# Graph network, layer 2: maximum in place, four-node pieces, longer gaps, and three engines in written order

## The chip, the cores and the metric

The kernel runs on one core of one Trainium2 chip. The metric is the device time of one execution in microseconds (us); the figure for a kernel is the median of its runs. The core has five engines, each with an instruction queue of its own: TensorE (PE in the profile, with its weight loads as PEld), VectorE (DVE), ScalarE (ACT), GpSimd (POOL) and SyncE (SP). DMAs are issued by SP, ACT and POOL.

## The reference, cut to what matters

Four graph layers run on N = 6250 nodes (49 tiles of 128) with E = 100000 edges (782 groups of 128), sorted by destination. The input is normalised, and the result is added to it at the end.

```python
h = jnp.maximum(_layernorm(x), 0.0)
msum = segment_sum(h[src], dst)                                        # layer 1: mean
h = h @ W1_self + (msum / clip(deg, 1)) @ W1_neigh + b1
hp = relu(h @ W2_pool + b2_pool)                                       # layer 2: maximum
hmax = where(deg > 0, segment_max(hp[src], dst), 0.0)
h = h @ W2_self + hmax @ W2_neigh + b2
h = ((segment_sum(h[src], dst) + h) / (deg + 1)) @ W3_neigh + b3       # layer 3: gcn
h = h @ W4_self + (segment_sum(h[src], dst) / clip(deg, 1)) @ W4_neigh + b4
out = x + h @ W_fc + b_fc
```

The destinations are skewed: low node numbers have far more edges than high ones.

## The kernel before

The kernel has a fast path, timed here, and a general path that runs only when a flag says that the graph doesn't fit the fast one. Because the layers after the maximum are linear, the fast path folds the weights of layers 2 to 4 together; `W3_neigh`, `W4_*` and `W_fc` are multiplied into products of 256 or 512 columns, and layers 3 and 4 only add up rows.

Neighbour sums of layers 1, 3 and 4 are done in two ways. For the tiles of nodes with many edges (hub tiles, numbers 0 to `HUB`: 8, 16 or 18 by layer) the adjacency is a dense table `A` of small counts, multiplied by the rows on TensorE (`dense`, L489). For the others the edges are gathered 128 at a time and added up by one-hot products (`sums`). `build` makes the dense tables: nodes are taken in windows of `WIN = 8`; each group of up to 128 edges of a window becomes two one-hot matrices, `hs` (source within its tile; two ScalarE operations, L319 and L321) and `hm` (source tile and node of the window; VectorE, L323), whose product (L329) counts the edges. Windows of tiles 0 to 7 are built during layer 1, those of tiles 8 to 17 during layer 2, with two groups of edges each. After a layer-2 window's last product ScalarE runs over it twice: `many` (L337) looks whether a count exceeds 15 and L339 copies it into `A` as fp8. `Hub` holds such a list of work, makes the one-hots `LOOK = 4` ahead, and is moved on by `advance`.

Layer 2 is one long loop over the 782 groups of edges, in six blocks (`BLOCKS`), the last block first. In each step POOL gathers 128 rows of 512 floats by source (L1240) into half of a buffer `X` (six buffers of two halves), and VectorE keeps a running maximum along the edges of each lane (L1247), into two PSUM tiles `run0` and `run1` in turn. Of each pair one row is kept: a third VectorE operation makes it (L1283), and it is stored to DRAM (L1288). After a block `carry` joins the runs that cross from one lane to the next.

Beside this, in every step, the loop moves on several things, all in Python generators whose `yield` gives the turn back until the next step:

- `products2`, the weight folding: 28 pieces, from step 9 one per step. A piece of `product` loads 128 rows of weights (`wl`, issued by ScalarE), transposes them on TensorE (L259), copies them (L260), multiplies (L263) and copies the result (L265).
- `chains` and `node_rows`: keys for `carry` and, per block, the rows at which each node's maximum will lie.
- `hub.advance`: the windows of tiles 8 to 15 until step 250, of 16 and 17 after.
- `done2`, one per tile of nodes whose blocks are complete: gathers the maxima (`totals`, L1149), transposes, multiplies by the folded weights (L1173, L1176, L1179), adds the bias row `prow` (L1183) and writes the row in three bf16 parts (`parts`) to `tab_r`.
- `early`: the products of layer 3 with tiles 6 to 37 of `tab_r`, in batches of four tiles, that can be made already here; their sums go to `acc3` (`add3`, L1040).

The order in which an engine issues its instructions is chosen by a scheduler when the kernel is built: it works from the dependencies and its own estimate of durations, and may move instructions past one another. Once built, each engine's queue is fixed.

Of the kernel before, what the change touches and what calls it, by code (L numbers as in the profile page):

```python
# [20 lines left out]
P = 128  # L21
# [8 lines left out]
WIN = 8  # L30
# [48 lines left out]
def fast_path(  # L79
# [59 lines left out]
    WT = P // WIN  # L139
    NW = WT * H4  # L140
    assert H1 <= H3 <= H4 and NW + 1 <= 3 * P
    k_of = [math.ceil(_edges_between(w * WIN, (w + 1) * WIN, E, N) / P) for w in range(NW)]
    assert all(p >= q for p, q in zip(k_of, k_of[1:]))
    row_of, spans = {}, []
    nrow = 0
    for w0, w1_ in ((0, WT * H1), (WT * H1, NW)):
# [72 lines left out]
    most = const.tile([P, NW], F32, name="most")  # L219
# [86 lines left out]

    def build(d, A, keys, pool, psb, plain=True):

        sk, mk, r0 = keys
        work = []  # L310
        for w in range(d * WT, (d + 1) * WT):
            hold = {}
            for k in range(k_of[w]):
# [12 lines left out]
                def run(k=k, w=w, hots=hots, hold=hold):  # L326
# [4 lines left out]
                    if k == k_of[w] - 1:  # L331
                        c = (w % WT) * WIN
                        if plain:
                            nc.vector.tensor_reduce(most[:, w : w + 1], hold[0], AX.X, ALU.max)
                        else:
                            many = pool.tile([P, NT * WIN], BF16, name="many", bufs=1)
                            nc.scalar.activation(many, hold[0], AF.Relu, bias=less,  # L337
                                                 accum_out=most[:, w : w + 1])
# [8 lines left out]

    LOOK = 4

    class Hub:  # L350


        def __init__(self, work=()):
# [23 lines left out]
        def advance(self, to):  # L377
            while self.done < min(to, len(self.work)):
                if self.work[self.done][0]:
                    self.passed += 1  # L380
                while self.hot < min(self.passed + LOOK, len(self.hot_at)):
                    self.work[self.hot_at[self.hot]][0]()
                    self.hot += 1
# [194 lines left out]
    with ExitStack() as pro:  # L578
# [67 lines left out]
        for r, w0, n, k in spans:  # L646
# [6 lines left out]
        sel_at = (0, RB1, RB1)  # L653
        sel = [ep.tile([P, n], F32, name=f"sel{c}")
               for c, n in enumerate((RB1, RB * P - RB1, RB * P - RB1))]

        def select(c):
# [8 lines left out]
        iota_n = ep.tile([P, 3 * P], F16, name="iota_n")  # L666
        nc.gpsimd.iota(iota_n, pattern=[[WIN, 3 * P]], base=0, channel_multiplier=0,
                       allow_small_or_imprecise_dtypes=True)
        SN = ep.tile([P, 3, 2], F32, name="SN")
        nc.gpsimd.iota(SN[:, :, 1], pattern=[[WIN * P, 3]], base=0, channel_multiplier=WIN,  # L670
                       allow_small_or_imprecise_dtypes=True)
        dlast = ep.tile([P, 1], F32, name="dlastf")
        nc.vector.tensor_copy(dlast, dstI[:, T - 1 : T])
        under = ep.tile([P, 3 * P], BF16, name="under")
        nc.vector.tensor_scalar(under, iota_n, dlast, None, op0=ALU.is_gt)
        pc = bank(psm, "pm", "pc_c", (3,))
        for c in range(3):
            nc.tensor.matmul(pc[:, c : c + 1], under[:, c * P : (c + 1) * P], ones_b,
                             start=True, stop=True)
        cF = ep.tile([P, 3], F32, name="cF")  # L680
        nc.vector.tensor_scalar(cF, pc, float(P - 1), None, op0=ALU.min)
        cI = ep.tile([P, 3], I32, name="cI")
        nc.vector.tensor_copy(cI, cF)
        within = ep.tile([P, 3], F32, name="within")
# [28 lines left out]
        def check_room():  # L713

            pr_ = bank(psm, "pm", "pr_s", (3 * P,))
            for c in range(3):
                nc.tensor.matmul(pr_[:1, c * P : (c + 1) * P], SN[:, c, 0:1], ident,
                                 start=True, stop=True)
            starts = ep.tile([1, 3 * P], F32, name="starts")
# [40 lines left out]
        def window_keys(sk, mk):  # L760
# [5 lines left out]
            nc.vector.scalar_tensor_tensor(mk[:, c], mk[:, c], float(WIN) / P, dw[:, c],  # L766
                                           op0=ALU.mult, op1=ALU.add)
            nc.vector.tensor_scalar(dw[:, c], dw[:, c], float(WIN), 1024.0, op0=ALU.is_ge,
# [88 lines left out]
        window_keys(sk1, mk1)  # L857
        select(1)
        select(2)
        begins(1)  # L860
        begins(2)
        row_begins(RB1 // P, RB, (1, 2))
# [20 lines left out]
        window_keys(skR, mkR)  # L883
# [69 lines left out]
    def node_rows(pool, psm):  # L953
# [28 lines left out]
        for b, tb in enumerate(BLOCKS):  # L982
# [6 lines left out]
            nc.vector.tensor_mul(q, q, ok)  # L989
            nc.vector.tensor_scalar(pI, q, 1.0 / tb, None, op0=ALU.mult)  # L990
# [17 lines left out]
            nc.vector.tensor_add(t_, t_, pF)  # L1008
            nc.vector.tensor_scalar(t_, t_, float(run_at[b]), None, op0=ALU.add)
# [35 lines left out]
    with tc.tile_pool(name="fl2c", bufs=1) as ck, ExitStack() as late:  # L1045
# [3 lines left out]
        psb = late.enter_context(tc.tile_pool(name="psb2", bufs=1, space=PSUM))  # L1049
# [4 lines left out]
        prow = ck.tile([P, FH], F32, name="prowf")  # L1054
# [26 lines left out]
        def products2(wp):  # L1081
# [7 lines left out]
            b4r = wp.tile([P, FO], F32, name="b4rf")  # L1089
            b2r = wp.tile([P, FH], F32, name="b2rf")  # L1090
# [22 lines left out]
        def carry(b, last):  # L1113
# [3 lines left out]
            yield  # L1117
            cT = wk.tile([P, KH, P], F32, name="cTf", bufs=1)
# [8 lines left out]
            yield  # L1127
            pc = bank(psm, "pm", "pcf")
            for k in range(KH):
                nc.tensor.transpose(pc[:, k * P : (k + 1) * P], cT[:, k, :], ident)  # L1130
            for _ in range(4):
                yield
# [5 lines left out]
            for _ in range(4):  # L1138
                yield
# [18 lines left out]
        def done2(d):  # L1158
            tots, th = totals(d)
            for _ in range(4):  # L1160
                yield
# [5 lines left out]
            for j in range(KH):  # L1167
                nc.tensor.transpose(pt[:, j, :], hm[:, j * P : (j + 1) * P], ident)
            hT = wk.tile([P, KH, P], F32, name="hTf")
            nc.scalar.copy(hT, pt)  # L1170
            pm = bank(psm, "pm", "pm_prf")
# [10 lines left out]
            pr = wk.tile([P, FH], F32, name="prf")  # L1182
# [17 lines left out]
        early_pool = []  # L1200

        def early_products():
# [3 lines left out]
            for d in range(H3):  # L1206
                got = {}

                def load(d=d, got=got):
# [5 lines left out]
                             lambda s: batch[s], FH, psd, lambda v, d=d: add3(d, v))  # L1215
                early.add([(load, work[0])] + work[1:])
# [4 lines left out]
        A = wk.tile([P, NT, P], F8, name="A", bufs=1)  # L1221
        first, rest = (
            [w for d in ds for w in build(d, A, (skR, mkR, RB1), wk, psb, False)]
            for ds in (range(H1, H3), range(H3, H4))
        )
        hub = Hub(first + rest)
        tiles, begun2 = [], 0
# [3 lines left out]
        for b in reversed(range(NB)):  # L1231
            tb = BLOCKS[b]
            t0 = offs[b] // P
            prev = None
            for s0 in range(0, tb, G2):
                n = min(G2, tb - s0)
                X = (xmore if at // G2 % 2 else xpool).tile([P, G2, FH], F32, name="X2")
                for k in range(n):
# [5 lines left out]
                    if s0 + k:  # L1244
                        run = (X[:, k, :] if s0 + G2 >= tb
                               else psr.tile([P, FH], F32, name=f"run{k}"))
                        nc.vector.scalar_tensor_tensor(  # L1247
                            run, prev, same[:, t : t + 1], X[:, k, :],
                            op0=ALU.mult, op1=ALU.max,
# [828 lines left out]
```

## Time and profile before

| | |
|---|---|
| median of 3 runs | 3320.49 us (3316.07 to 3323.73) |
| the profiled execution | 3354.4 us |
| its span in the profile | 3352.6 us |
| mean granted TensorE clock | 0.885 |
| busy: PE, DVE, ACT, POOL | 2515.0, 2178.8, 993.2, 1948.2 us |
| HBM traffic | 806 MB, mean 240 GB/s |
| layer 1 (with the start), layer 2, layers 3 and 4 | about 0 to 910, 910 to 2335, 2335 to 3352 us |

The profile is of one execution. "Busy" is the time in which an engine executed instructions other than register, branch, semaphore and DMA-issuing ones. A line of a group gives: source line, engine, operation, output and inputs, shape, count, busy us, mean ns of one, and then the idle time of the engine just before them with what ended most of it. "issue" means that the engine waited for nothing that the profile shows. In the tables of windows each engine's busy time is followed by its number of instructions, and the last three columns are the granted TensorE clock as a share of full speed, the mean busy share of the 16 DMA engines, and GB/s.

### The profile page before, as it was taken

The page shows a single profiled execution, that of the slowest core. Times are in us where ns is not written, and L with a number is a line of the kernel's source. Part 1 is how long each engine was busy: PE and PEld are TensorE (multiplying, and loading weights), DVE is VectorE, ACT ScalarE, POOL GpSimd, SP SyncE. Part 2 cuts the span into 40 slices and gives each one's busy share as a digit, 9 for nine tenths or more (in the row PEclk, how much of TensorE's full clock was granted, in tenths as well). Part 3 has the DMA queues.
Part 4 walks back from the last instruction along what each step waited for, and adds up shares of the span by engine and source line. Part 5 has one row for each costly group of instructions (what it writes and reads, how often), then busy time and mean ns, then how long its engine had stood idle before and what let it go on. Part 6 is the DMA issues. An engine that isn't in the chain of part 4 may idle for free.

```text
span 3352.6 us, 39513 instructions
## 1 busy us (share of the span) xinstructions
PE 2515.0 (75%) x11395; PEld 1293.9 (39%) x11523; DVE 2178.8 (65%) x5588; ACT 993.2 (30%) x2703; POOL 1948.2 (58%) x2255
## 2 busy tenths in 40 slices
PE   4557888889776555588888923872889999888887
PEld 2134556556443222233333411331333333444444
DVE  7845555655378778677777886785456656355555
ACT  4845555553256787322111110000000001000000
POOL 4266656666455555555565666563666665566664
PEclk9678989999887676789989966986999999999999
DMA  5455656666688788788888888886999998666675
GB/s 175 150 150 150 171 168 178 180 189 181 193 276 260 251 266 280 257 282 270 277 282 277 285 283 263 268 280 208 366 325 328 340 323 298 214 197 198 202 205 170
DMA packets 350368, 806.06 MB, mean 240 GB/s; under 512 B 55694, under 2 KB 147318, under 8 KB 350108
## 3 DMA queue, kind: packets, MB, share of 16 engines
q0 software_dynamic: 146080, 513.65, 50.2%
q1 hardware_dynamic: 145976, 234.34, 19.2%
q10 hardware_dynamic: 58084, 55.44, 5.4%
q8 instruction: 93, 1.52, 0.2%
q14 instruction: 135, 1.11, 0.1%
HBM read 604.85 MB, written 199.17 MB: 240 GB/s over the span
## 4 chain that ended last, share of the span: by engine, by line
PE 55%; issue 13%; DVE 11%; ACT 7%; DMA 7%; another core or an unknown queue 5%; POOL 3%; ACTq 0%; DVEq 0%; POOLq 0%; SPq 0%
PE pd L489 15%; PE pg L433 10%; PE pd L484 5%; DVE run L1247 3%; PE pd L485 3%; PE pb L329 3%; PE pm_prf L1179 3%; PE pm_hp L928 3%; PE pm_hp L931 2%; PE pm_w L263 2%; PE pm_prf L1173 2%; PE pg L428 2%; DVE X L1283 2%; ACT hs L321 2%
## 5 line engine op out<-in xcount | busy, mean ns | idle before, releaser
L1240 POOL DMA_INDIRECT X<-rows,srcIf x782 | 755.3, 966 | 565.8 <-issue 212.5
L411 POOL DMA_INDIRECT ring<-tab_h,srcT x474 | 452.5, 955 | 280.7 <-issue 99.0
L433 PE MATMUL pg<-ring,hot 128*128 128x512 bf16 (+2 forms) x2431 | 532.3, 329 | 82.8 <-issue 34.4
L1247 DVE SCALAR_TENSOR_TENSOR run<-run,samef,X 128x512 f32<-128x512 f32 x758 | 571.6, 754 | 34.1 <-DMA X<-rows,srcIf 11.5
L462 DVE SCALAR_TENSOR_TENSOR acc<-pg,M,acc 128x256 f32<-128x256 f32 (+2 forms) x694 | 356.4, 538 | 150.8 <-PE pg L433 48.5
L411 POOL DMA_INDIRECT ring<-tab_r,srcE x342 | 332.9, 973 | 194.4 <-issue 80.4
L329 PE MATMUL pb<-hm,hs 128*128 128x392 bf16 x781 | 262.5, 380 | 223.2 <-ACT A L339 96.4
L489 PE MATMUL pd<-r,ae 128*128 128x512 bf16 x1494 | 368.9, 395 | 66.7 <-DVE acc L1040 41.1
L411 POOL DMA_INDIRECT ring<-tab_s,srcE x314 | 301.4, 960 | 187.9 <-PE pg L429 68.6
L321 ACT ACTIVATE hs<-ht,onef 128x128 bf16<-128x128 bf16 x781 | 293.5, 397 | 348.5 <-PE pb L329 128.1
L433 PEld LDWEIGHTS <-hot 128*128 128x128 bf16 x2448 | 245.8, 101 | 328.5 <-issue 183.9
L407 DVE TENSOR_SCALAR hot<-iota_bf,keyE 128x128 bf16<-128x128 bf16 x656 | 159.6, 272 | 260.5 <-PE pg L429 101.9
L484 PE MATMUL pd<-zt,ac 128*128 128x512 bf16 x835 | 300.0, 388 | 25.9 <-issue 23.7
L1283 DVE SCALAR_TENSOR_TENSOR X<-X,samef,run 128x512 f32<-128x512 f32 x379 | 279.6, 738 | 0.0
L485 PE MATMUL pd<-zt,ac 128*128 128x256 bf16 x882 | 245.1, 278 | 29.3 <-issue 26.8
L489 PEld LDWEIGHTS <-ae 128*128 128x128 fp8e4 x1536 | 155.2, 101 | 288.5 <-issue 141.9
L489 PE MATMUL pd<-zt,ac 128*128 128x512 bf16 x797 | 229.2, 386 | 24.0 <-issue 14.7
L407 DVE TENSOR_SCALAR hot<-iota_bf,keyT 128x128 bf16<-128x128 bf16 x474 | 119.9, 265 | 169.8 <-PE pb L329 51.5
L489 PE MATMUL pd<-Z,A 128*128 128x256 bf16 (+1 forms) x1176 | 195.2, 282 | 26.5 <-issue 10.1
L329 PEld LDWEIGHTS <-hs 128*128 128x128 bf16 x781 | 82.3, 106 | 286.3 <-issue 207.1
L1179 PE MATMUL pm_prf<-unf,hTf 128*128 128x512 f32 x392 | 189.0, 608 | 4.5 <-issue 4.4
L323 DVE TENSOR_SCALAR hm<-iota_w,mk 128x392 bf16<-128x392 f16 x461 | 150.0, 340 | 53.2 <-PE pb L329 23.9
(329 smaller groups left out, 3559.7 us busy)
## 6 DMA issues: line engine op xcount, KB each, us to landing
rows<-X SPq DMA_DIRECT2D x385, 256.0 KB
tab_r<-r SPq DMA_DIRECT2D x49, 384.0 KB
tab_a<-A SPq DMA_DIRECT2D x18, 784.0 KB
tab_t<-th SPq DMA_DIRECT2D x49, 256.0 KB
rows<-hpf SPq DMA_DIRECT2D x49, 256.0 KB
th<-tab_t ACTq DMA_DIRECT2D x49, 256.0 KB
X<-rows,srcIf POOLq DMA_INDIRECT x782
ac<-tab_a ACTq DMA_DIRECT2D x90, 112.0 KB
```

The costliest lines, as they stand in the source:

```text
L321: nc.scalar.activation(hots[0], t, AF.Relu, bias=one, scale=-1.0)
L329: nc.tensor.matmul(hold[0], hots[0], hots[1], start=(k == 0), stop=(k == k_of[w] - 1))
L411: nc.gpsimd.indirect_dma_start(out=ring[:, j % deep, :], out_offset=None, in_=table, in_offset=bass.IndirectOffsetOnAxis(ap=srcT[:, j - jb ...
L433: nc.tensor.matmul(pg[:, : F + c], hot[j], X[:, part * F : (part + 1) * F + c], start=(k == 0 and part == 2), stop=(k == n - 1 and part == 1),
L462: nc.vector.scalar_tensor_tensor(acc[d], half, m, acc[d], op0=ALU.mult, op1=ALU.add)
L484: nc.tensor.matmul(hold[0], a, z[:, : 2 * F], start=(s == ss[0]), stop=False)
L485: nc.tensor.matmul(hold[0][:, :F], a, z[:, 2 * F :], start=False, stop=(s == ss[-1]))
L489: nc.tensor.matmul(hold[0][:, : F + c], a, z[:, part * F : (part + 1) * F + c], start=(s == ss[0] and part == 2), stop=(s == ss[-1] and pa ...
L1179: nc.tensor.matmul(pm, hT[:, c, :], un[:, c, :], start=False, stop=(c == KH - 1))
L1240: nc.gpsimd.indirect_dma_start(out=X[:, k, :], out_offset=None, in_=tab_p, in_offset=bass.IndirectOffsetOnAxis(ap=srcI[:, t : t + 1], axis=0),
L1247: nc.vector.scalar_tensor_tensor(run, prev, same[:, t : t + 1], X[:, k, :], op0=ALU.mult, op1=ALU.max,)
L1283: nc.vector.scalar_tensor_tensor(X[:, 0, :], X[:, 1, :], same[:, t : t + 1], before, op0=ALU.mult, op1=ALU.max,)
```

## The change

Everything is about layer 2, except that the start of the kernel makes the keys for the smaller windows.

1. The running maximum is kept in one PSUM tile per block, updated in place; the kept row of a pair is made between the two updates. The freed PSUM bank goes to the window products (`psb2` gets two).
2. The windows of tiles 8 to 17 have four nodes (`WIN2`) and one group of edges each: 320 products of 196 columns instead of 392. `hs` is finished for four windows in one operation, two windows share a PSUM tile and one copy to `A`, the look for counts over 15 is taken from `A` in four pieces per tile, and one-hots are made 12 ahead. The copies are issued one pair later. The start of each window is found by a further group of `select`, `begins` and products.
3. The bias row `prow` is no longer added to each tile but to `qrow`, which is added after layer 3 has divided by `deg + 1`. The tile's three parts are made straight from PSUM.
4. `node_rows`, `carry` and `done2` yield more often between instructions of different engines; a new tile begins at the earliest 11 steps after the one before; sums of early products are taken in one product chain later (`take_sums`); `early` drains by a 32nd per step instead of a 40th.
5. From the start of the loop to the end of layer 2, VectorE, ScalarE and TensorE issue their instructions in the order in which they are written.

```diff
-WIN = 8
+WIN, WIN2 = 8, 4
...
+    def build_narrow(d, keys, pool, psb, copies):
...
+            def hot(r=r, v=v):
+                i = v % 4
+                if i == 0:
+                    held["ht"] = pool.tile([P, 4, P], BF16, name="ht", bufs=2)
+                nc.scalar.activation(held["ht"][:, i, :], iota_b, AF.Abs, bias=sk[:, r : r + 1])
+                hm = pool.tile([P, NT * WIN2], BF16, name="hm", bufs=16)
+                nc.vector.tensor_scalar(hm, iota_w[:, : NT * WIN2], mk[:, r : r + 1], None,
+                                        op0=ALU.is_equal)
+                held["hm", v] = hm
+                if i == 3:
+                    hs = pool.tile([P, 4, P], BF16, name="hs", bufs=5)
+                    nc.scalar.activation(hs, held["ht"], AF.Relu, bias=one, scale=-1.0)
+                    held["hs", v // 4] = hs
...
+                def copy(pb=pb):
+                    c = (v - 1) * WIN2
+                    nc.scalar.copy(
+                        A[:, :, c : c + 2 * WIN2].rearrange("p s (i c) -> p i s c", c=WIN2),
+                        pb.rearrange("p (i s) c -> p i s c", s=NT), saturate=True)
+                    if v == WT2 - 1:
+                        nc.sync.dma_start(tab_a[d], A.bitcast(BF16))
+
+                def look(n):
+                    s0, s1 = LOOKS[n]
...
+                    nc.scalar.activation(many[:, : s1 - s0, :], A[:, s0:s1, :], AF.Relu,
+                                         bias=less, accum_out=most[:, at : at + 1])
+
+                if i == 1:
+                    for f in copies[:2]:
+                        f()
+                    del copies[:2]
+                    copies.insert(0, copy)
...
-        psb = late.enter_context(tc.tile_pool(name="psb2", bufs=1, space=PSUM))
+        psb = late.enter_context(tc.tile_pool(name="psb2", bufs=2, space=PSUM))
...
-            yield from bias_rows(psm, b1c, us, prow)
-            yield from bias_rows(psm, b2c, V, b2r)
-            nc.vector.tensor_add(prow, prow, b2r)
+            yield from bias_rows(psm, b1c, us, b1r)
+            yield from bias_rows(psm, b2c, V, b2r, b1r)
             yield from bias_rows(psm, b4c, wfc, b4r, bfc)
-            yield from bias_rows(psm, b3c, B4, qrow)
+            yield from bias_rows(psm, b3c, B4, qrow, b2r)
...
         def done2(d):
             tots, th = totals(d)
-            for _ in range(4):
+            for _ in range(6):
                 yield
...
+            yield
+            yield
+            yield
+            r3 = early_pool[0].tile([P, 3 * FH], BF16, name="r3", bufs=2 * BATCH + 1)
+            hi, mid, lo = (r3[:, i * FH : (i + 1) * FH] for i in range(3))
+            nc.scalar.copy(hi, pm)
+            yield
+            yield
+            if d < H3:
+                add3(d, pm)
             pr = wk.tile([P, FH], F32, name="prf")
-            nc.vector.tensor_add(pr, pm, prow)
-            yield
-            if d < H3:
-                add3(d, pr)
-            r3 = early_pool[0].tile([P, 3 * FH], BF16, name="r3", bufs=2 * BATCH + 1)
-            parts(pr, FH, r3)
+            nc.vector.tensor_sub(pr, pm, hi)
+            yield
+            nc.scalar.copy(mid, pr)
+            yield
+            yield
+            nc.vector.tensor_sub(lo, pr, mid)
...
-                             lambda s: batch[s], FH, psd, lambda v, d=d: add3(d, v))
-                early.add([(load, work[0])] + work[1:])
+                             lambda s: batch[s], FH, psd, lambda v, d=d: summed.append((d, v)))
+
+                def then(w):
+                    take_sums()
+                    w()
+
+                early.add([(load, work[0])] + [lambda w=w, i=i: then(w) if i == len(work) - 2 else w()
+                                               for i, w in enumerate(work[1:])])
...
+        in_order.enter_context(tc.manual_schedule(engines={mybir.EngineType.DVE, mybir.EngineType.Activation, mybir.EngineType.PE}))
...
-        hub = Hub(first + rest)
+        hub = Hub(first + rest, 12)
+        def step(put, held, st, row):
+            nc.vector.scalar_tensor_tensor(put, held, st, row, op0=ALU.mult, op1=ALU.max)
...
+            run = psr.tile([P, FH], F32, name="run")
...
-                    if s0 + k:
-                        run = (X[:, k, :] if s0 + G2 >= tb
-                               else psr.tile([P, FH], F32, name=f"run{k}"))
-                        nc.vector.scalar_tensor_tensor(
-                            run, prev, same[:, t : t + 1], X[:, k, :],
-                            op0=ALU.mult, op1=ALU.max,
-                        )
...
+                    row, st = X[:, k, :], same[:, t : t + 1]
+                    if s0 + G2 >= tb:
+                        step(row, X[:, 0, :] if k else run, st, row)
+                        if k:
+                            stored(b, s0 // 2, X)
+                    elif k == 0 and s0:
+                        step(run, run, st, row)
+                    elif k:
+                        held = run if s0 else X[:, 0, :]
+                        if s0 == 0:
+                            step(run, held, st, row)
+                        step(X[:, 0, :], row, st, held)
+                        if s0:
+                            step(run, run, st, row)
+                        stored(b, s0 // 2, X[:, :1, :])
...
-                    early.advance(early.done + math.ceil(early.left() / 40))
+                    early.advance(early.done + math.ceil(early.left() / 32))
...
-                    if tiles and not ends and begun2 < NT * (at - FIRST_AT) / (T - 20 - FIRST_AT):
+                    if (tiles and not ends and at >= begun_at + 11
+                            and begun2 < NT * (at - FIRST_AT) / (T - 20 - FIRST_AT)):
```

More of the change, by code (lines that the diff above doesn't have):

```diff
@@ L332, in run @@
                         c = (w % WT) * WIN
[L333 to L338, printed above, removed]
+                        nc.vector.tensor_reduce(most[:, w : w + 1], hold[0], AX.X, ALU.max)
                         nc.scalar.copy(A[:, :, c : c + WIN],
@@ L346, in build, with run @@
         return work
+    def build_narrow(d, keys, pool, psb, copies):
+        sk, mk, r0 = keys
+        work = []
+        held = {}
+        for v in range(WT2):
+            r = row_of[NW1 + (d - H1) * WT2 + v, 0] - r0
+            def hot(r=r, v=v):
[11 more added lines that the diff above has]
+                    held["hs", v // 4] = hs
+            def run(v=v):
+                if v == 0:
+                    held["A"] = pool.tile([P, NT, P], F8, name="A", bufs=2)
+                A = held["A"]
+                i = v % 2
+                if i == 0:
+                    held["pb"] = bank(psb, "pb", "pb", (2 * NT, WIN2))
+                pb = held["pb"]
+                nc.tensor.matmul(pb[:, i * NT : (i + 1) * NT, :].rearrange("p s c -> p (s c)"),
+                                 held["hs", v // 4][:, v % 4, :], held.pop(("hm", v)),
+                                 start=True, stop=True)
+                def copy(pb=pb):
[7 more added lines that the diff above has]
+                    s0, s1 = LOOKS[n]
+                    at = NW1 + len(LOOKS) * (d - H1) + n
+                    many = pool.tile([P, 13, P], BF16, name="many", bufs=1)
+                    nc.scalar.activation(many[:, : s1 - s0, :], A[:, s0:s1, :], AF.Relu,
[5 more added lines that the diff above has]
+                    copies.insert(0, copy)
+                    if v == WT2 - 1:
+                        copies.extend(lambda n=n: look(n) for n in range(len(LOOKS)))
+            work.append((hot, run))
+        return work
@@ L1138, in carry @@
             for _ in range(4):
+                yield
+            pc = bank(psm, "pm", "pcf")
+            for k in range(KH):
+                nc.tensor.transpose(pc[:, k * P : (k + 1) * P], cT[:, k, :], ident)
+            for _ in range(3):
                 yield
@@ L1200, in fast_path, with take_sums @@
         early_pool = []
+        summed = []
+        def take_sums():
+            while summed:
+                add3(*summed.pop(0))
         def early_products():
@@ L1304, in fast_path @@
                     now.remove(g)
+        for f in copies:
+            f()
         early.advance(len(early.work))
-        nc.vector.tensor_scalar(most[:, : H1 * WT], most[:, : H1 * WT], less, None, op0=ALU.add)
+        take_sums()
+        in_order.close()
+        nc.vector.tensor_scalar(most[:, :NW1], most[:, :NW1], less, None, op0=ALU.add)
         nc.vector.tensor_reduce(bad[:, 3:4], most, AX.X, ALU.max)
```

130 lines of the change are left out of this document (65 added, 65 removed).

## The prediction

> **What bounds the kernel now.** I read the busy times by stage first. Layer 2's gather loop runs from about 909 to 2301 us of the span, and no engine is full in it:
>
> ```profile
> 913.00:1043.00 130.00, 101.24 (x347) 55.11 (x346) 100.47 (x272) 73.93 (x210) 71.57 (x77) 0.91 0.85 282
> 1043.00:1480.00 437.00, 261.70 (x725) 111.92 (x727) 341.26 (x752) 281.67 (x849) 247.93 (x255) 0.74 0.82 265
> 1480.00:1960.00 480.00, 404.21 (x1470) 182.03 (x1496) 378.25 (x606) 94.11 (x229) 278.57 (x290) 0.93 0.84 276
> ```
>
> Columns: length; busy us of PE, PEld, DVE, ACT, POOL; granted clock, DMA share, GB/s. Finer windows, same columns:
>
> ```profile
> 1160.00:1210.00 50.00, 26.62 (x68) 10.22 (x67) 44.24 (x88) 45.03 (x142) 27.81 (x29) 0.67 0.84 272
> ...
> 2160.00:2210.00 50.00, 49.68 (x197) 23.08 (x199) 47.74 (x71) 4.23 (x7) 31.01 (x33) 1.00 0.89 287
> ```
>
> ```profile
> 1990.00:2000.00 10.00, 0.00 (x0) 0.00 (x0) 8.77 (x14) 0.00 (x0) 7.55 (x9) 0.50 0.95 312
> ```
>
> Early, ACT and DVE are the fullest (45 and 44 of 50 us); later PE and DVE; with PE idle, POOL gathers back to back, 1.25 us apart, at 312 GB/s. Last, the page's groups:
>
> ```profile
> L1240 POOL DMA_INDIRECT X<-rows,srcIf x782 | 755.3, 966 | 565.8 <-issue 212.5
> ...
> L1247 DVE SCALAR_TENSOR_TENSOR run<-run,samef,X 128x512 f32<-128x512 f32 x758 | 571.6, 754 | 34.1 <-DMA X<-rows,srcIf 11.5
> ...
> L1283 DVE SCALAR_TENSOR_TENSOR X<-X,samef,run 128x512 f32<-128x512 f32 x379 | 279.6, 738 | 0.0
> ```
>
> POOL idles 566 us before 782 gathers. Some 0.30 us each is issue (235 us); the other 330 us are waits, mostly for X buffers that DVE has not emptied, and DVE in turn waits for PE and ACT. By the counts of L1247 (28 by 960 us, 31 more by 1010) DVE is at gather step 40 at about 980 us; it ends step 782 at 2301. That is 1,321 us for 742 steps, **1.78 us a step**.
>
> **The change, part by part.** The *in-place maximum* keeps three operations of 0.74 to 0.75 us per pair of gathers: nothing saved on DVE, one PSUM bank freed, which the window products get.
>
> *Four-node pieces* keep 320 one-hot products in layer 2. ACT: 316 hs of 402 ns (118 us) become 80 over 512 columns, 49 us at the 616 ns of the 128x512 cast (L296); 160 `many` with their reads (94 + 32 us) become 40 looks over up to 1,664 elements. No row has that size: the 128x128 and 128x392 activations (402 and 586 ns) give 0.70 ns an element, so 1.7 us each with the read, 67 us (between that and 126, if it saved nothing). Together 128 us off ACT. DVE: hm over 196 columns instead of 392 lies between the 265 ns of the 128x128 `hot` and 329; 285 taken, 14 us off. PE: between nothing and half of 103 us off. Nothing ends on these alone, but ACT, among the fullest until 1360 us, falls clear of the bound.
>
> *Bias in qrow*: 49 additions of 686 ns leave DVE (34 us), into its idle time. *Longer gaps* add no work; a tile finishes about ten steps later, which only the last tile shows, and the end drains without steps: nothing, at most one 0.7 us addition. *Prologue*: a fourth group of window starts adds one `drow` gather on a single buffer; the chain of waits has 3.55 us of DMA for one and 1 us of DVE. Between 0 and 6 us, **+3** taken, because DVE is full (10 of 10 us) from 80 to 150 us.
>
> *Written order* cuts both ways.
>
> (a) At the start it costs. The folding of the weights, 28 pieces, is written one per step in steps 9 to 36; so far the scheduler could spread it. In order DVE can't get past it: `rl` waits for PE's transposes of the step before (steps 9 to 20), `beg` for PE at step 22, and from step 21 the ring of 16 hm, 12 looked ahead, lets DVE be some 4 steps ahead of PE. The maxima queue behind these on DVE, the X buffers and POOL behind the maxima. So DVE is at step 40 when PE ends step 36. PE's piece:
>
> ```profile
> 1013.67 5.40 PE L263 MATMUL pm_w<-Vf,wT 128*128 128x512 f32 x8 [3.43 <-ACT wT L260]
> ...
> 1020.23 3.70 PE L263 MATMUL pm_w<-Vf,wT 128*128 128x512 f32 x8 [0.39 <-issue]
> ...
> 1025.09 3.70 PE L263 MATMUL pm_w<-usf,wT 128*128 128x512 f32 x8 [0.40 <-issue]
> ```
>
> Starts are 4.86 us apart. In written order a step's window work on ACT (ht 0.4, a quarter of hs, half a copy of A: 0.85 us) stands between one piece's copy and the next `wT`: 5.7. Eight 256-wide pieces at 3.3 (as from 937 to 951 us), sixteen at 5.7, bias rows 13, the first 13 window one-hots 6 at once: 137 us from 912, where the first piece starts. Step 40 comes at 1049 instead of 980, **+69 us** (60 to 85).
>
> This needs the weights early. Their load is issued by ACT and written behind a copy that waits for PE:
>
> ```profile
> 1023.97 0.59 ACT L265 COPY usf<-pm_w 128x512 f32<-128x512 f32 x1 [1.67 <-issue]
> 1024.41 0.33 ACTq L255 DMA_DIRECT2D wl<-in_L_gnn_W_neigh  x1
> 1024.45 0.59 ACT L260 COPY wT<-pt_w 128x512 f32<-128x512 f32 x1
> ```
>
> The load starts while the copy before it still runs, and just ahead of `wT`, so ACT's queue issues loads beside its own work; which of them was written first the trace does not show. The Trainium skill ("Perfetto Trace Analysis", Sequencer Loop) says that a sequencer pushes an engine instruction into a queue, where it waits for its semaphores, and reads on. By that rule a load is not held by a waiting copy and (a) is +69; against it, the first rival's +179.
>
> (b) Later it gains. Afterwards no engine waits for an order the scheduler guessed wrongly: DVE's early sums come one product chain later, casts two steps later. What remains is throughput. A gather and half a store are 384 KB; a tile adds 256 (th), 1.16 x 256 (tot) and 384 (tab_r), 71 KB a step at one tile per 13.3 steps; early blocks and tab_a some 22. These 477 KB at 312 GB/s are 1.57 us a step. DVE in the window from 2160 needs 47.7 us for 33 gathers, 1.45; PE there 1.51. PE's share is uneven: the early hub now takes 2 items a step while over 32 are left, so of the 53 steps between batches 16 hold 2 x 0.69 us (three L489 of 0.23) and 0.68 for tiles, 2.06 in all. Were that rigid, the mean would be (16 x 2.06 + 37 x 1.57) / 53 = 1.72; were it elastic, 1.57. I take 1.64 for the 492 steps with tiles and early products, 1.57 for the other 250: 1,199 us, **-122 us**.
>
> Sum: 3 + 69 - 122 = **-50 us**. The profiled execution took 3354.4 us (span 3352.6 and 1.8 around it), 1.0% over the median of 3320.5; a difference of 50 changes by half a us with that, so the forecast is 3270. Its own range: 1.52 to 1.70 us a step throughout, and 60 to 85 at the start, 3190 to 3348.
>
> **The rivals.** *The weight loads are held back.* Each then starts after the copy that waits for its predecessor's product. A 512-wide piece becomes 5.0 (between 3.70 and the 5.40 after a pause) + 0.95 for that copy and window work + 0.33 issue + 3.0 landing (2.0 for `rows<-fixf` in the quiet end, up to 7.9 for `th`) + 1.4 for transposes and `wT`, 10.7 us; a narrow one, with 2.9 of PE and no window work, 7.9. 63 + 171 + 13 = 247 us put step 40 at 1159, +179 for +69: 3 + 179 - 122 = +60, **3380**. It decides from 8.2 us for a wide piece (5.4 for a narrow one), where start and gain cancel. For it: the written order; against it: the row at 1024.41. The Trainium skill ("TensorE: Matmul & The Clock Gate", Part 1) halves PE's clock after some 3.4 us of idleness; 5.40 after 3.43 us of waiting agrees, and by it alone the sum would be 6 us higher.
>
> *Order stalls take the place of order stalls*: each engine's waits now stop all behind them, and the step stays at 1.78. 3 + 69, **3392**. For it: DVE, PE and ACT wait for each other in turn in the trace; against it: the written gaps.
>
> *The pace reaches the floor*: DMA showed 350 GB/s at a share of 1.00 (1210 to 1220 us), 1.40 us a step; with PE's 1.51 on the 492 steps 1.47 in all. 3 + 69 - 230, **3162**.
>
> *Only the smaller instructions count*, the order being much the same: DVE's 48 us, a quarter of it on the path, **3308**.
>
> **How the numbers follow.** Forecast 0.47; loads held back 0.23; new order stalls 0.17; floor 0.08; order without effect 0.05. A measurement of this kernel tells 0.2% (7 us) from no change. Faster: most of the forecast's range (0.41), floor, half of the last, and a sliver of the held loads where the pace is good, 0.54. Same: 0.05. Slower: 0.41. The range leaves out half of the floor case, and the outer part of the two slow ones: 3180 to 3395.
>
> **What would show it.** Right: L1240 with clearly less idle time waiting for DVE; ACT under 1 us a step until step 250; from step 40 to the end some 1,200 us at about 300 GB/s; pieces of the weight folding one after the other on PE, DVE and POOL nearly still beside them for some 70 us longer than now. The first rival shows as PE waiting for `DMA wl` before every transposition and step 40 near 1160; the second as DVE idle behind PE's L489 or ACT's casts all through 1300 to 2200. I am wrong if step 40 is not late at all, or if DMA passes 330 GB/s over a whole stage.

## The result, and the profile after

The changed kernel takes 3514.68 us (median, 3498.93 to 3527.57) where the kernel before took 3320.76 beside it: 1.0568 times as long, 95% interval 1.0539 to 1.0596. The forecast was 3270. The profiled execution has a span of 3519.2 us, 166.6 more than before, at a granted clock of 0.865. Source lines are those of the changed kernel.

First the stages of the gather loop, as tables of windows with the columns of the prediction:

```profile
913.00:1043.00 130.00, 73.42 (x173) 41.72 (x174) 27.92 (x80) 22.10 (x50) 24.66 (x27) 0.65 0.32 103
1043.00:1200.00 157.00, 85.22 (x213) 37.19 (x211) 69.60 (x252) 53.95 (x119) 27.49 (x29) 0.77 0.31 96
...
1480.00:1960.00 480.00, 324.64 (x1107) 147.99 (x1106) 350.31 (x581) 107.92 (x220) 287.17 (x302) 0.83 0.85 282
2160.00:2210.00 50.00, 32.68 (x123) 13.85 (x121) 45.95 (x74) 3.10 (x6) 33.53 (x36) 0.85 0.94 306
```

Before, the window from 913 to 1043 had VectorE busy for 100 us and DMA at 282 GB/s; now it is 28 us and 103 GB/s, and DMA stays at 96 GB/s until 1200. From 1480 to 1960 VectorE (350 us, before 378) and DMA (282 GB/s, before 276) are nearly as before. The page's groups that answer to those of the prediction:

```profile
L1338 POOL DMA_INDIRECT X<-rows,srcIf x782 | 745.6, 953 | 721.8 <-issue 220.3
...
L1319 DVE SCALAR_TENSOR_TENSOR run<-run,samef,X 128x512 f32<-128x512 f32 x758 | 571.8, 754 | 42.0 <-DMA X<-rows,srcIf 15.9
...
L1319 DVE SCALAR_TENSOR_TENSOR X<-X,samef,run 128x512 f32<-128x512 f32 x379 | 282.0, 744 | 36.6 <-issue 16.2
```

POOL's idle time before the gathers rose from 566 to 722 us; the maxima cost what they did. And the timeline of a piece of the folding (start, duration, engine, line, operation, then the idle time before it and what ended it):

```profile
949.02 0.37 ACT L269 COPY B4f<-pm_w 128x256 f32<-128x256 f32 x1 [3.87 <-PE pm_w L267]
949.08 0.34 ACTq L259 DMA_DIRECT2D wl<-in_L_gnn_W_neigh  x1
...
952.27 0.96 PE L263 MATMUL pt_w<-identf,wl 128*128 128x128 f32 x4 [3.29 <-DMA wl<-in_L_gnn_W_neigh]
...
953.96 3.78 PE L267 MATMUL pm_w<-wfcf,wT 128*128 128x256 f32 x8 [0.73 <-ACT wT L264]
...
958.21 0.29 DVE L1136 COPY rl<-rowsf 128x128 f32<-128x128 f32 x1 [14.24 <-PE rowsf L1132]
...
987.40 6.66 PE L267 MATMUL pm_w<-B4f,wT 128*128 128x512 f32 x8 [0.73 <-ACT wT L264]
```

The load goes out 0.06 us after the copy that waited 3.87 us for the product before; TensorE waits 3.29 us more for it to land; and VectorE stands 14.24 us at `rl` behind TensorE, its maxima behind that.

To place the loss I list the starts of POOL's 782 gathers. POOL runs up to twelve gathers ahead of VectorE (six buffers of two halves), so gather 64 starts after the folding in every kernel that folds one piece a step. In the profiled executions:

| kernel | gather 9 | gather 64 | 9 to 64 | gather 782 | us a step, 64 to 782 |
|---|---|---|---|---|---|
| before | 913 | 1008 | 95 | 2295 | 1.79 |
| changed | 913 | 1200 | 287 | 2461 | 1.76 |

So the start loses **192 us** and the other 718 steps gain **26**; the difference of the two, 166, is the difference of the spans. Part of the 26 may be work done sooner: of the row keys (`nr`) VectorE does 33.8 us before gather 64, where the kernel before does 7.6 (913 to 1200 against 913 to 1008).

### The profile page after: what moved, and what is told of

The parts are those of the page before. It is cut to its first block, busy times and chain, and to the rows that moved or that the text cites. A ratio compares the mean times of both kernels' runs of the same rounds, so it can differ in the third digit from the quotient of the medians.

```text
span 3519.2 us, 39061 instructions
## 1 busy us (share of the span) xinstructions
PE 2548.5 (72%) x11532; PEld 1316.6 (37%) x11532; DVE 2150.6 (61%) x5544; ACT 924.3 (26%) x2223; POOL 1944.3 (55%) x2257
## 5 line engine op out<-in xcount | busy, mean ns | idle before, releaser
L1338 POOL DMA_INDIRECT X<-rows,srcIf x782 | 745.6, 953 | 721.8 <-issue 220.3
L492 PE MATMUL pg<-ring,hot 128*128 128x259 bf16 (+1 forms) x2448 | 530.9, 328 | 70.8 <-issue 39.0
L548 PE MATMUL pd<-r,ae 128*128 128x512 bf16 x1536 | 391.7, 402 | 125.6 <-DVE acc L1105 43.3
L543 PE MATMUL pd<-zt,ac 128*128 128x512 bf16 x882 | 316.0, 388 | 27.8 <-issue 22.3
L548 PE MATMUL pd<-zt,ac 128*128 128x512 bf16 x816 | 230.3, 382 | 22.2 <-issue 13.9
L377 PE MATMUL pb<-hm,hs 128*128 128x196 bf16 x320 | 79.6, 300 | 217.0 <-ACT A L382 86.8
L325 ACT ACTIVATE hs<-ht,onef 128x128 bf16<-128x128 bf16 x461 | 174.5, 394 | 162.6 <-PE pb L333 77.3
L333 PE MATMUL pb<-hm,hs 128*128 128x392 bf16 x461 | 159.0, 371 | 59.6 <-ACT hs L325 26.1
```

The source lines that it names most:

```text
L325: nc.scalar.activation(hots[0], t, AF.Relu, bias=one, scale=-1.0)
L333: nc.tensor.matmul(hold[0], hots[0], hots[1], start=(k == 0), stop=(k == k_of[w] - 1))
L492: nc.tensor.matmul(pg[:, : F + c], hot[j], X[:, part * F : (part + 1) * F + c], start=(k == 0 and part == 2), stop=(k == n - 1 and part == 1),
L543: nc.tensor.matmul(hold[0], a, z[:, : 2 * F], start=(s == ss[0]), stop=False)
L548: nc.tensor.matmul(hold[0][:, : F + c], a, z[:, part * F : (part + 1) * F + c], start=(s == ss[0] and part == 2), stop=(s == ss[-1] and pa ...
L1338: nc.gpsimd.indirect_dma_start(out=X[:, k, :], out_offset=None, in_=tab_p, in_offset=bass.IndirectOffsetOnAxis(ap=srcI[:, t : t + 1], axis=0),
```

## The experiments

They ran in four groups of four kernels, each with runs of the kernel before on the same chip: 2928 us (e1 to e4), 3361 (e5 to e8), 3330 (e9 to e12) and 2930 (e13 to e16). The first and the last group ran on one chip, where the kernel before takes 12 to 13% less time than on the two chips of the other groups. So each ratio is to the kernel before of its own group, and kernels of different groups are compared where that one's time is alike. The changed kernel itself was measured on the slower chips alone.

| kernel | ratio to before, 95% interval | 9 to 64, us | us a step, 64 to 782 |
|---|---|---|---|
| **before: 3330 to 3361 us** | | | |
| e6 before | 1 | 99 | 1.80 |
| e5 changed kernel | 1.0570 (1.0522 to 1.0617) | 296 | 1.76 |
| e12 loads early | 1.0279 (1.0237 to 1.0322) | 192 | 1.74 |
| e9 no order | 0.9951 (0.9928 to 0.9974) | 94 | 1.74 |
| e10 order from step 64 | 1.0030 (1.0001 to 1.0059) | 92 | 1.76 |
| e11 the same, even spread | 0.9950 (0.9922 to 0.9977) | 96 | 1.75 |
| e7 no order, old maximum | 0.9945 (0.9917 to 0.9973) | 96 | 1.77 |
| e8 no order, old gaps | 0.9941 (0.9907 to 0.9974) | 99 | 1.75 |
| **before: 2928 to 2930 us** | | | |
| e1 loads early | 1.0228 (1.0206 to 1.0250) | 183 | 1.51 |
| e2 order from step 64 | 0.9864 (0.9842 to 0.9885) | 76 | 1.53 |
| e3 no order | 0.9721 (0.9700 to 0.9742) | 74 | 1.47 |
| e4 VectorE and TensorE ordered | 1.0130 (1.0108 to 1.0151) | 166 | 1.51 |
| e13 loads early, pieces spread | 1.0142 (1.0114 to 1.0170) | 107 | 1.59 |
| e14 the same, even spread | 1.0044 (1.0028 to 1.0059) | 111 | 1.55 |
| e15 VectorE alone ordered | 1.0007 (0.9993 to 1.0021) | 165 | 1.47 |
| e16 order from step 64, short gaps | 1.0352 (1.0311 to 1.0392) | 75 | 1.73 |

**Which half of the start is the loads?** e1, e12 and e5:

```diff
+            def fetch():
+                while len(loaded) < 3:      # wl: 3 buffers
+                    w, m = next(loads, (None, 0))
+                    ...
+                        nc.scalar.dma_start(loaded[-1], w[m * P : (m + 1) * P, :])
+                return loaded.pop(0)
```

> The changed kernel, but each of the 28 weight loads of layer 2's folding is written two pieces ahead, so that it stands on ScalarE in front of the copies that wait for TensorE. Theory A (the start is lost because each load stands behind a copy that waits for the product before it: landing and issue, 3.2 to 3.6 us, are paid once a piece): 28 x 3.5 = about 100 us come back, step 40 at 1050 to 1080 us instead of 1167, 3400 to 3425 us. Rival (the lockstep of VectorE, TensorE and ScalarE in written order costs the time, the loads are hidden anyway): step 40 stays past 1140, 3490 to 3515 us.

> The changed kernel once more, on the chip of this group, so that the experiments can be set against it: the first four showed the kernel before at 2928 us instead of 3320. If the loss at the start is a wait for loads (a delay that depends little on how fast the bulk moves), it stays near 190 us by step 64 and the ratio to before rises to about 1.055 to 1.07 (3090 to 3130 us). If the loads are not the cause, it is no slower than the kernel with early loads, about 2995 us.

> The changed kernel with the loads two pieces early, beside the others on one chip. Held loads: step 64 is 190 to 200 us late in the changed kernel where the kernel before takes 3320 to 3360 us; early loads take 28 x 3.3 = 92 us off, step 64 about 1110 us, and the lockstep of the folding keeps the other 100. Rival (loads hidden): 1195 us or more.

On one speed of chip, 9 to 64 takes 296 us in the changed kernel, 192 with early loads, 94 without order (e5, e12, e9): **104 us are the loads, 98 something else**. e5 and e12 came out as expected. (The expectations count 28 loads; the loop has 24, since four of the 28 pieces are bias rows.) In the changed kernel's waits of TensorE (us in total, times, longest us), 913 to 1200:

```profile
PE pt_w L263 <- DMA wl<-in_L_gnn_W_neigh: 45.2, 14, 6.0
PE pt_w L263 <- DMA wl<-in_L_gnn_W_self: 22.4, 8, 6.3
```

That is 68 us. Most of the rest is TensorE's clock, 0.65 of full speed from 913 to 1043 (before, 0.91): the eight narrow products, of 256 columns, take 3.78 us, not 1.99 as in most of them before, and the sixteen wide ones, of 512, 24.6 us more in all than at 3.70. Together that is 39 us, of which the kernel with early loads keeps about 8: 68 + 31 = 99 of the 104. In its timeline (e12):

```profile
986.20 0.58 ACT L272 COPY Vf<-pm_w 128x512 f32<-128x512 f32 x1 [3.79 <-PE pm_w L270]
986.21 0.33 ACTq L1169 DMA_DIRECT2D wl<-in_L_gnn_W_neigh  x1
986.99 0.58 ACT L267 COPY wT<-pt_w 128x512 f32<-128x512 f32 x1
...
987.62 3.70 PE L270 MATMUL pm_w<-Vf,wT 128*128 128x512 f32 x8 [0.93 <-ACT wT L267]
```

The load still leaves with the copy, 0.01 us after its start, but it is one for two pieces on, and no later piece of the folding waits for its load. e1's total in us can't be set against its expectation, which was worked out from the slower chip's times; e12 answers it there, 3422 us for 3400 to 3425. Moving the load cured the wait; whether ScalarE's sequencer or its queue holds an issue behind a waiting copy no run separates.

**What is the other half?** e4, e13, e14, e15. The edits: the set of ordered engines without ScalarE (e4), with VectorE alone (e15); for e13 and e14, on top of early loads,

```diff
-                        next(steps, None)
+                        if at % 3 == 0:
+                            next(steps, None)
```

with `MADE_AT` 96, and for e14 (and e11) an even spread:

```diff
-                    early.advance(early.done + math.ceil(early.left() / 32))
+                    early.advance(early.done + 1 + (at % 4 == 0))
```

> The changed kernel with the written order on VectorE and TensorE alone; ScalarE's instructions, the weight loads among them, are put in order by the scheduler. Theory A: the loads can move ahead, step 40 at 1040 to 1090 us, 3390 to 3430 us with the later pace unchanged. Rival (lockstep of VectorE and TensorE): 3480 us or more. If ScalarE's queue also sets the later pace (a cast that waits holds the copies behind it), the step after 1160 us falls from 1.75 to under 1.68 us, another 50 us.

> The changed kernel with written order on VectorE alone; TensorE and ScalarE in the scheduler's order, so loads and folding pieces can move. If VectorE's own order is what ties the loop to the folding (it waits for rows and window keys in turn): start loss 60 us or more, ratio 1.01 to 1.03. If it needs the order of TensorE or ScalarE too: start as without order, 0.995 to 1.005 (0.97 to 0.99 where before takes 2930 us).

> The changed kernel, loads two pieces early, and the 28 folding pieces every third step (steps 9 to 92) in place of every step. If VectorE is tied to the pace of the pieces: a piece of 5.7 us every three steps is 1.9 us a step, little above the 1.75 of the loop, so about 13 us remain of the 100, 1.00 to 1.01 times the kernel before where that takes 3320 to 3360 us (about 0.99 to 1.00 where it takes 2930). If something else of the order at the start costs: still 1.02 to 1.03 (both chips).

> The same with the early blocks at 1.25 items a step. The even spread took 0.8% off before (1.003 to 0.995), so 0.992 to 1.002 if the two add; no change from the one before if the pieces, not the early blocks, hold the pace.

With VectorE alone in order (e15) the start is 165 us long, 91 more than without (e3), and no more with TensorE added (e4, 166): VectorE's own order is enough. e15's loss at the start was expected, its ratio (1.0007) was not, since the pace falls to 1.47 afterwards. e4 does not show the later gain that its expectation allowed for: its pace, 1.51, is that of e1, where ScalarE is in order. VectorE's waits in e12, 907 to 1109:

```profile
DVE rl L1139 <- PE rowsf L1135: 25.6, 4, 15.8
DVE b2rf L282 <- ACT b2rf L280: 22.6, 1, 22.6
DVE hm L364 <- PE pb L380: 15.8, 6, 3.9
DVE nr L1033 <- PE ps_n L1032: 13.3, 1, 13.3
DVE rl L1139 <- PE pt_w L266: 10.7, 1, 10.7
```

These 88 us are keys of the chains, row keys, window one-hots and the bias rows, each behind a piece of the folding on TensorE, with the maxima queued behind them. They are not all of order's making. The windows from gather 9 to 64, e12 and then e9:

```profile
917.00:1109.00 192.00, 118.47 (x384) 63.09 (x384) 98.07 (x335) 75.05 (x170) 52.43 (x56) 0.83 0.48 149
```

```profile
910.00:1004.00 94.00, 60.83 (x241) 37.70 (x240) 64.42 (x156) 53.77 (x129) 52.23 (x57) 0.86 0.83 279
```

VectorE is idle for 94 us instead of 30, so order adds 64 us of waiting; the other 34 of the 98 are work, 30 of them row keys (33.6 us against 3.9), which the kernel without order does after gather 64.

e13 missed its expectation (0.99 to 1.00): gather 64 came early, but gather 100 at 1016 us, against 930 in e3 and 1036 in e1, 2.4 us a step from gather 9 on. VectorE now waits for the pieces through the ring of hm:

```profile
DVE hm L364 <- PE pb L380: 43.9, 16, 6.9
```

I had set 1.9 us a step and left out the windows' own copies, for which TensorE's window products wait 46.5 us in the same stretch. e14 missed its range with e13 (1.0044 for 0.992 to 1.002), though the even spread took 25 us off.

**Does order pay once the folding is done?** e2, e3, e9, e10, e11. e2 and e10 enter the written order at step 64; e3 and e9 delete it.

> The changed kernel, but the written order begins only after step 64, when the folding is done. Theory A or any theory by which the whole loss comes from the order during the folding: step 40 at 980 us as before, and with the pace of 1.75 us a step of the changed kernel 3320 to 3340 us. Rival (the loss comes from the longer gaps, the pieces or the maxima, whatever the order): over 3450 us. If the order after step 64 also gains as predicted (1.61 us a step), 3230 us.

> The changed kernel without any written order; pieces, maxima, gaps and bias stay. If the order alone makes the loss: start as before, and VectorE's and ScalarE's smaller load worth 10 to 40 us, 3280 to 3320 us. If longer gaps and pieces cost by themselves: over 3340 us. Compared with the kernel whose order begins after step 64 it tells what the order is worth later: predicted 122 us in its favour, by the second rival nothing.

> The changed kernel without written order again, to stand on one chip with the next three. With the kernel before at about 2930 us: 0.972 as before. With it at about 3320 to 3360 us (as in the measurement of the change): with the old maximum or the old gaps it was 0.994 there, so 0.98 to 0.994; below 0.99 if maximum and gaps each bring a part, 0.994 if neither does.

> Written order from step 64 on. If the order costs later too (1.5% more than no order on the faster chip: VectorE waits 35 us for TensorE's early products in steps 500 to 782, against 4), this is 1 to 1.5% above the kernel without order. If the later order helps where transfers are slow, at or below it.

> Written order from step 64 on, with the early blocks spread at 1.25 items a step in place of two a step and then one. The prediction gave 1.72 us a step for a rigid order (16 steps at 2.06, 37 at 1.57) and 1.57 for an elastic one. If the order is rigid and the uneven spread is what it costs: 20 to 45 us faster than written order with the old spread, VectorE's wait for L548 below 15 us in steps 500 to 782. If something else in the order costs (casts, sums, gathers of tiles): within 8 us of it.

It does not. Order from step 64 costs 44 us on the faster chip (2891 against 2847) and 17 on the slower one (3337 against 3320, 0.5% where e10 expected 1 to 1.5). The totals expected of e2 and e3 were worked out from the slower chip too; e10 and e9 answer them there, 3337 us for 3320 to 3340 and 3320 for 3280 to 3320, so nearly the whole loss comes with the order during the folding. VectorE's waits between gathers 64 and 782, the largest two of e2 (first) and the first of e3 with the one on TensorE:

```profile
DVE acc L1105 <- PE pd L548: 41.9, 18, 3.3
DVE run L1318 <- DMA X<-rows,srcIf: 38.5, 34, 3.8
```

```profile
DVE run L1318 <- DMA X<-rows,srcIf: 32.8, 31, 2.6
...
DVE acc L1105 <- PE pd L548: 4.5, 12, 1.3
```

In written order VectorE takes a sum where it is written, and waits 41.9 us for early products that TensorE gets in bursts of two a step; in the scheduler's order the same wait is 4.5 us. With the even spread e11 is 22 us below e10 (20 to 45 expected; the wait falls from 43.5 to 17.4 us) and e14 25 below e13 (from 39.7 to 13.0): in written order the uneven spread has a price. With TensorE out of the order as well as ScalarE (e15) the wait is 6.8 us, where e4 has 40.0, and the pace is 1.47 again.

**Do the other parts do anything?** e6 to e8 and e16: e7 and e8 put back the old maximum (with its PSUM banks) and the old gaps, sums and spread in the kernel without order; e16 puts the old `yield`s of `done2` and `carry` into e2.

> The kernel before, for its profile on the chip of this group: step 64 near 885 us and a later step of 1.55 to 1.60 us, if the pace of the loop follows the rate of the transfers (1.78 us at about 280 GB/s, 1.47 to 1.53 us at about 320 in the kernels without order during the folding).

> The changed kernel without written order, with the running maximum of before (two PSUM banks for it, one for the window products). If the in-place maximum brings nothing, as the prediction says, the ratio to before stays at 0.972 (within 0.3%). If the second bank of the window products, or one operation less between a gather and its free buffer, is what gains, the ratio goes back to 0.98 to 1.00.

> The changed kernel without written order, with the short gaps of before: the tile's steps, the carry, the sums and the spread of the early blocks as they were (the casts stay on the new path without the bias row). By the prediction the gaps cost and gain nothing where no order is imposed: ratio 0.972. If the gaps are where the gain of the kernel without order comes from (VectorE, TensorE and ScalarE wait less for each other in the scheduler's order too): 0.985 to 1.00.

> Written order from step 64 on, with the short gaps of before in the tile's steps and in the carry. If the longer gaps are what makes written order bearable: VectorE waits for casts and products at every tile (about 59 tiles times 2 to 4 us), 1.02 to 1.05 where the long gaps gave 1.003 (1.01 to 1.03 where they gave 0.986). If the gaps do nothing under order either: within 0.4% of those values.

Without order neither the maximum nor the gaps tell (0.9945, 0.9941, and 0.9951 with both parts, in e9; one within the other's interval, on the slower chips). Under order the gaps are worth 4.9 points (1.0352 against 0.9864), more than I allowed for. VectorE's waits in e16 from gather 64 on:

```profile
DVE prf L1252 <- ACT r L1248: 144.6, 31, 11.7
DVE acc L1105 <- ACT r L1248: 81.6, 14, 10.0
```

226 us behind the tiles' casts, where e2 has 13.6 at the larger of the two rows. The kernel before took 1.80 us a step in e6, not 1.55 to 1.60, since that group ran on the slower chip.

**What sets the pace?** The same kernel without order ran at 1.47 us a step (e3) and at 1.74 (e9). Windows from gather 64 to 782, e3 and then e9:

```profile
871.00:1929.00 1058.00, 818.36 (x2925) 372.05 (x2923) 960.59 (x1814) 329.86 (x701) 745.25 (x778) 0.87 0.96 331
```

```profile
1004.00:2252.00 1248.00, 860.58 (x2946) 385.60 (x2944) 966.28 (x1826) 336.53 (x718) 740.94 (x779) 0.84 0.86 281
```

VectorE's work is the same to 6 us, but on the slower chip it is idle for 273 us instead of 89, and of these 141 have no releaser that the profile knows ("issue" and "remote"), against 2. One of them in the timeline of e9:

```profile
1680.79 0.81 PE L548 MATMUL pd<-r,ae 128*128 128x512 bf16 x3
...
1686.59 0.69 DVE L1105 TENSOR_TENSOR acc<-acc,pd 128x512 f32<-128x512 f32 x1 [7.42 <-issue]
...
1687.33 3.14 PE L548 MATMUL pd<-r,ae 128*128 128x512 bf16 x7 [5.73 <-DVE acc L1105]
```

TensorE's recorded products end at 1681.6; the sum that needs them starts 5 us later, together with a load issued by SP. POOL issues gathers until 1685.5. What holds TensorE's signal there stays open; a product without a record would look the same.

## Why the prediction was wrong

- **Written order at the start, +69 us: wrong by the loads; the lockstep was seen, but mis-sized.** The failed step is "a load is not held by a waiting copy". The working took it from the row at 1024.41, where a load started while the copy before it ran, and from the rule of the Trainium skill ("Perfetto Trace Analysis", Sequencer Loop) that a sequencer reads on past a waiting engine instruction. That row fits both readings: the load starts 0.05 us after the transposes end that read its buffer, of which there were two, so the buffer may have set its time.

```profile
1023.76 0.60 PE L259 MATMUL pt_w<-identf,wl 128*128 128x128 f32 x4
```

  In the changed kernel's trace the load starts just after the copy does, 0.06 us at 949.02, and never while the copy waits: of the 24 loads all but the first start 0.01 to 0.07 us after the instruction written before them. For a DMA issued by ScalarE the traces here disagree with the rule. The first rival had the start right: 10.3 us between wide products against its 10.7, 8.5 between the last six narrow ones against 7.9, VectorE's step 40 at about 1170 against 1159.

  With early loads the wide pieces go at 5.8 us from the fourth on (5.7 predicted), and the bias rows take TensorE 13 us, as put. But the start loses 98 us, for 60 to 85: in e12 the 28 pieces and the one-hots among them take TensorE 151 us instead of 137 (the narrow ones 40 for 26, the first three wide ones 25 for 17), and the row keys, done sooner, were not in the sum. The prologue's 3 us can't be told from noise: gather 9 starts at 913 us in both profiles, at 912 in e6 (before) and 915 in e5 (changed).
- **Later pace, 1.57 to 1.64 us a step, -122: wrong; 1.76 and -26.** The failed step is "afterwards no engine waits for an order the scheduler guessed wrongly". Of VectorE's idle time from gather 64 to 782, all rows of the waits summed, 264 us before and 297 after, 149 and 177 name no releaser ("remote" and "issue"). VectorE's work in this stretch fell by 61 us (1012 to 952), 20 of them row keys done sooner, but its idle time rose by 35 (the rows leave out the shortest gaps), which leaves the 26. The largest rows of VectorE's waits, before and then after:

```profile
DVE acc L1040 <- remote: 47.3, 14, 7.9
DVE prf L1183 <- remote: 27.8, 4, 11.0
DVE hm L323 <- remote: 24.0, 7, 8.8
```

```profile
DVE acc L1105 <- remote: 73.0, 11, 11.6
DVE prf L1261 <- ACT r L1255: 45.6, 9, 13.4
```

  The rows were there to be read: 149 us over 718 steps are 0.21 us a step, as much as lies between the forecast's 1.57 and the 1.78 of before; that it is the same time is not shown. No run on the slower chips removed them (134 to 177 us in every profile there), and where they come from stays open. What written order could have taken away was smaller, and it put waits of its own in their place (casts 66 us of VectorE's waits, before 16), which is the second rival. That rival's pace, 1.78, and the first one's start, 179, give 3 + 179 = 182 over the kernel before; the medians differ by 194. That the sum comes so near is partly luck, since its parts were 192 and -26 in the profiles. I had let each rival fail one step while the other held; both failed.
- **The floor, 1.47 us a step,** was met on the faster chip alone, by e3 without order (DMA 0.96 busy at 331 GB/s) and by e15 with VectorE alone in order (0.96, 329 GB/s).
- **In-place maximum, 0: right without order** (e7). **Gaps, 0: right without order** (e8), but under order they are what keeps it bearable (e16).
- **Pieces and bias:** ScalarE's one-hots and looks fell by 61 and 54 us, 115 for 128 (the 512-wide `hs` takes 722 ns, not 616; a look 1.57 to 1.68 us and 0.19 for its read, as estimated); hm takes 278 ns for 285. The fourth rival, the order without effect, gave 3308, 0.4% below the median of before: without order the kernel is 0.5% below (e9), and 2.8% below on the faster chip. Which part makes that 2.8% was not told apart.
- **Written order as a whole** is the loss: on the slower chips the kernel takes 0.9951 of the time of before without it (e9) and 1.0570 with it (e5). On the faster chip it takes 0.9721 without it, and every variant with order takes longer than that.

## What to carry over

When instructions are put in written order, go through each ordered queue and ask of every instruction that waits what stands behind it, DMAs included: an issue that starts just after a waiting instruction may have been held by it, and it belongs in front. Before a gain is read from an engine's idle time, split that time by what ended it, and leave out what has no name: none of the reorderings here removed it. Order on VectorE alone already tied it to the folding on TensorE, for 91 us. Longer written distances made order cheaper (e2 against e16), but not a gain (e2 against e3).

## What was not expected of the hardware

One chip ran the kernel before in 2928 to 2930 us, two others in 3330 and 3361. Between gathers 64 and 782 the kernel without order had 2 us of unnamed idle time on VectorE on the first and 141 on the second, at 331 and 281 GB/s. And a ScalarE-issued load, written behind a copy that waited, left 0.01 to 0.06 us after the copy's start in the rows shown, not before.
